# A four-layer kernel on one core: small TensorE groups placed one tile of the code search behind their producers

## The chip, the cores and the metric

The kernel runs on one core of a Trainium2 chip. The metric is the device time of one execution in microseconds (us). A core has five engines that matter here, each with its own queue, worked through in order: TensorE (PE, with PEld for its weight loads), VectorE (DVE), ScalarE (ACT), GpSimd (POOL) and SyncE (SP), which issues DMAs. Engines wait for each other by semaphores. An instruction that waits holds up everything behind it on its engine.

## What is computed

The input x has 16 images of 64 x 64 tokens with 256 channels. Four layers follow, each of the form x = x + L(group norm of x); the group norm has 32 groups of 8 channels and takes its mean and variance over a whole image.

```
L0: code search.  d = |x|^2 + |e|^2 - 2 x.e for 1024 codes e; take the nearest code's row
L1: per image row of 64 tokens: f = x Wf, g = x Wg, h = x Wh; out = sigmoid(f g^T) h
L2: x0, x1, x2 = x.w1, x.w2, x.w3 (one number a token);
    gate = sigmoid(sum_n x2[n] softmax_n(x0[n] x1[m]))[m]; out = gate * x
L3: linear attention with 4 heads of 32: softmax of q over a head, of k over the tokens,
    context = k^T v, out = layernorm(context q w_out)
```

## The kernel before

An image (4096 tokens, 256 channels as 2 halves of 128) is cut into 8 chunks of 512 tokens; the code search cuts a chunk into 4 tiles of 128 tokens, so an image has 32 tiles. Work on several images runs at once: while image b is searched, image b-1 is in layer 1, and earlier ones in layers 2 and 3. Each stage is a Python generator. A heap at the end of the kernel (function tile_net_kernel, at the foot) gives each generator a start in units of images and a length, and steps the one that is due; what a step yields is its share of the length. This makes the order in which instructions are *traced*. A scheduler then orders them by priority and by the buffers and engines that it takes to be free; a block under high_priority(offset=URGENT) goes ahead of what was traced up to 3000 places earlier. So the order on an engine is not the order of the text.

What the change and the prediction touch, with the lines of the kernel before:

- **gn_finish** (L259 to L282) closes a group norm. It runs four times an image: kind n0 (before the search), n1 (before layer 1), n2 (before layer 2), n3 (before layer 3), always under URGENT and in one step. DVE combines the statistics of the chunks into mv (L264). PE forms two sums in the bank pg (L268, L269) from the mean; ACT squares one into d (L271); PE forms the variance in pv from mv (L273) and from d (L274); ACT makes scale and nmean (s, L276; nm, L278); POOL raises s to the power -1/2 (L279) and forms nb (L281). For n0 three filler matmuls (function busy, L133) stand ahead of pg; their result is overwritten.
- **stage1**, the code search (L310 on). norm (L326) makes of a chunk, on ACT, the normalized tokens xn (L331) and their squares sq (L334): two instructions each. PE sums the squares over the channels into px (L340, 8 matmuls: four blocks of 32 partitions); ACT copies px to xrow (L345); PE turns xrow into pxt (L347), one transpose. norm_rows (L350) copies the four columns needed from pxt to nx2 on DVE (L352; nx in the profile). The search of a tile: ACT makes nn = -|e|^2 - |x|^2 (L381, from nx2); PE makes pd = 2 x.e, 1024 columns, in four matmuls (L386); DVE adds nn and takes the maximum into m8 (L392) and finds its place (L397); POOL gathers the code's row with an indirect DMA that adds it onto the tokens xc (L398). back (L357) transposes a chunk of the finished tokens (pt, L361), ACT copies it out (L364), DVE takes its statistics (L257). Within a chunk norm of the next chunk follows tile 2, norm_rows tile 3, and back of the last chunk tile 1.
- **rows2** (L550 on) prepares layer 2. Under URGENT, three filler matmuls (L133) go to the bank pbr, ACT scales the three weight vectors into wrow (L557), PE forms their bias (pbr, L562), ACT keeps it (L566). Then, for each half of the image, PE makes the three numbers of 2048 tokens in pr (L576), ACT adds the bias (rows, L580), ACT issues three DMAs that write them to DRAM, PE turns the rows (prt, L585: four transposes), and DVE copies two columns into x01 (L586; x_r in the profile). spread_rows (L591) loads the rows from DRAM, spread over the partitions, as x0b and x2b.
- **stage2** works on these: ACT's exponentials ex (L628, 2.09 us each) and DVE's weighted sums (L631, 2.32 us each), 64 of each an image. They are the costliest groups on their engines.
- layer1: ph (L476), psc, po (L516) on PE and the sum xt_l on DVE (L521). stage3: pk (L745), pqv (L762), ek, pc, pz (L835), pxo (L874) on PE.

Buffers: pd, ph and po share two double banks of PSUM; all other PSUM tiles share four single banks. Three SBUF buffers with the tag t4 are shared by nn, sq, fg of layer 1, and rows.

Of the kernel before, what the change touches and what calls it, by code (L numbers as in the profile page):

```python
# [41 lines left out]
def kernel(  # L42
# [212 lines left out]
    def chunk_stats(st, xt, ch):  # L255
        for k in range(NK):
            nc.vector.bn_stats(st[:, k, ch, :], xt[:, k, :])  # L257

    def gn_finish(st, kind, b):  # L259

        tag = f"{kind}_{b}"
        mv = small.tile([P, NK, 2], F32, tag="gn_mv", name=f"mv_{tag}")
        for k in range(NK):
            nc.vector.bn_aggr(mv[:, k, :], st[:, k, :, :].rearrange("p c s -> p (c s)"))  # L264
        mean = mv[:, :, 0]
        pg = bank(f"pg_{tag}")
        busy(pg, 3 if kind == "n0" else 0)
        nc.tensor.matmul(pg[:, 0:NK], lhsT=dmat, rhs=mean, start=True, stop=True)  # L268
        nc.tensor.matmul(pg[:, NK : 2 * NK], lhsT=gmat, rhs=mean, start=True, stop=True)  # L269
        d2 = small.tile([P, NK], F32, tag="gn_d", name=f"d_{tag}")  # L270
        nc.scalar.activation(d2, pg[:, 0:NK], AF.Square)  # L271
        pv = bank(f"pv_{tag}")
        nc.tensor.matmul(pv[:, 0:NK], lhsT=gmat, rhs=mv[:, :, 1], start=True, stop=False)  # L273
        nc.tensor.matmul(pv[:, 0:NK], lhsT=gmat, rhs=d2, start=False, stop=True)  # L274
        scale = small.tile([P, NK], F32, tag=f"gn_s{kind}", name=f"s_{tag}", bufs=3)
        nc.scalar.activation(scale, pv[:, 0:NK], AF.Identity, bias=eps5)  # L276
        nmean = small.tile([P, NK], F32, tag=f"gn_nm{kind}", name=f"nm_{tag}", bufs=3)
        nc.scalar.activation(nmean, pg[:, NK : 2 * NK], AF.Copy, scale=-1.0)  # L278
        nc.gpsimd.tensor_tensor(scale, scale, mhalf[:, 0:NK], ALU.pow)  # L279
        nbias = small.tile([P, NK], F32, tag=f"gn_nb{kind}", name=f"nb_{tag}", bufs=3)  # L280
        nc.gpsimd.tensor_tensor(nbias, nmean, scale, ALU.mult)  # L281
        return scale, nmean, nbias  # L282
# [9 lines left out]


    norm0 = {}

    def stats0(b):
# [3 lines left out]
        for ch in range(NCHUNK):  # L300
# [3 lines left out]
            yield 1.5  # L304
        with tc.high_priority(offset=URGENT):
            norm0[b] = gn_finish(st, "n0", b)
        yield 2
# [4 lines left out]
    def stage1(b):  # L312
# [3 lines left out]
        tok = x[b].rearrange("(t p) c -> p t c", p=P)  # L316
        xt, xc, xn, nx2, pxt = {}, {}, {}, {}, {}

# [8 lines left out]
        def norm(ch):  # L327
            xn[ch] = s1p.tile([P, NK, CW], F32, tag="xn", name=f"xn_{tag}_{ch}")
            sq = s1p.tile([P, NK, CW], F32, tag="t4", name=f"sq_{tag}_{ch}", bufs=3)
            for k in range(NK):  # L330
# [4 lines left out]
                    sq[:, k, :], xt[ch][:, k, :], AF.Square, bias=nbias[:, k : k + 1], scale=scale[:, k : k + 1]  # L335
                )
            px = bank(f"px_{tag}_{ch}")
            for t in range(CH):
                for k in range(NK):
                    nc.tensor.matmul(  # L340
                        px[32 * t : 32 * t + 32, :P], lhsT=neg32, rhs=sq[:, k, t * P : (t + 1) * P],
                        start=(k == 0), stop=(k == NK - 1),
                    )
            xrow = small.tile([P, P], F32, tag="xrow", name=f"xrow_{tag}_{ch}", bufs=1)
            nc.scalar.copy(xrow, px[:, :P])  # L345
            pxt[ch] = bank(f"pxt_{tag}_{ch}")
            nc.tensor.transpose(pxt[ch][:, :P], xrow, ident)  # L347

        def norm_rows(ch):
            px = pxt.pop(ch)  # L350
            nx2[ch] = small.tile([P, CH], F32, tag="x2", name=f"nx2_{tag}_{ch}")
            nc.vector.tensor_copy(nx2[ch], px[:, :P].rearrange("p (t n) -> p t n", n=32)[:, :, 0])  # L352
# [4 lines left out]
        def back(ch):  # L357
            for k in range(NK):
                pt = bank(f"pt_{tag}_{ch}_{k}")
                for t in range(CH):  # L360
                    nc.tensor.transpose(  # L361
                        pt[:, t * P : (t + 1) * P], xc[ch][:, t, k * P : (k + 1) * P], ident
                    )
                nc.scalar.copy(xt[ch][:, k, :], pt)  # L364
# [6 lines left out]
        load(1)  # L371
        norm(0)
        norm_rows(0)
        tokens(0)
        yield 4
        for ch in range(NCHUNK):
            for t in range(CH):
# [5 lines left out]
                for hf in range(2):  # L383
                    cols = slice(hf * 512, (hf + 1) * 512)
                    for k in range(NK):
                        nc.tensor.matmul(  # L386
                            pd[:, cols], lhsT=xn[ch][:, k, t * P : (t + 1) * P], rhs=e2[:, k, cols],
                            start=(k == 0), stop=(k == NK - 1),
                        )

# [12 lines left out]
                yield 4  # L403
                if t == 1 and ch > 0:
                    back(ch - 1)
                    yield 2
                if t == 2 and ch + 1 < NCHUNK:
                    norm(ch + 1)
                    yield 2
# [6 lines left out]
        back(NCHUNK - 1)  # L416
        with tc.high_priority(offset=URGENT):
            norm1[b] = gn_finish(st1, "n1", b)
        yield 3
# [4 lines left out]
    def layer1(b):  # L424
# [117 lines left out]

        with tc.high_priority(offset=URGENT):
            norm2[b] = gn_finish(st2, "n2", b)
        yield 2
# [4 lines left out]
    def rows2(b):  # L550
        tag = f"r2_{b}"
        scale, nmean, _ = norm2[b]
        with tc.high_priority(offset=URGENT):
            pb = bank(f"pbr_{tag}")
            busy(pb, 3)
            for k in range(NK):
# [3 lines left out]
                )  # L560
            for k in range(NK):
                nc.tensor.matmul(  # L562
                    pb[:, 0:1], lhsT=wrow_n[:, k, :], rhs=nmean[:, k : k + 1], start=(k == 0), stop=(k == NK - 1)
                )
            brow_n = small.tile([P, 1], F32, tag="brow_n", name=f"brow_{tag}")
            nc.scalar.activation(brow_n, pb[:, 0:1], AF.Identity, bias=brow)  # L566
        x01 = small.tile([P, NT, 2], F32, tag="x01", name=f"x01_{tag}", bufs=2)
        rd = dram.tile([3, 2, 4, CW], F32, tag="rows", name=f"rows_{tag}", bufs=3)
        for h in range(2):
            pr = bank(f"pr_{tag}_{h}")  # L570
            for j in range(4):
# [3 lines left out]
                for k in range(NK):  # L575
                    nc.tensor.matmul(  # L576
                        pr[part, :], lhsT=wrow_n[:, k, part], rhs=xt[:, k, :], start=(k == 0), stop=(k == NK - 1)
                    )
            rows = s1p.tile([P, CW], F32, tag="t4", name=f"rows_{tag}_{h}", bufs=3)
            nc.scalar.activation(rows, pr, AF.Identity, bias=brow_n)  # L580
            for n in range(3):
                nc.scalar.dma_start(out=rd[n, h], in_=rows[n : n + 97 : 32, :])
            pt = bank(f"prt_{tag}_{h}")
            for t in range(CH):
                nc.tensor.transpose(pt[:, t * P : (t + 1) * P], rows[:, t * P : (t + 1) * P], ident)  # L585
            nc.vector.tensor_copy(  # L586
                x01[:, 16 * h : 16 * h + 16, :].rearrange("p (j t) n -> p j t n", t=CH),
                pt.rearrange("p (t j n) -> p j t n", j=4, n=32)[:, :, :, 0:2],
            )
            yield 4  # L590
        rows_d[b] = x01, rd, [spread_rows(rd, b, 0)]  # L591
# [72 lines left out]
    def gate2(b):  # L664
# [9 lines left out]
        for ch in range(NCHUNK):  # L674
# [16 lines left out]
            nc.sync.dma_start(out=dst[ch], in_=xt)  # L691
        with tc.high_priority(offset=URGENT):
            scale, nmean, _ = gn_finish(st3, "n3", b)
        norm3[b] = scale, nmean, xm_
# [264 lines left out]
```

## Time and profile before

| | us |
|---|---|
| three runs | 5700.67, 5725.21, 5726.86 (median 5725.21) |
| the profiled execution | 5709.26 |
| its span | 5707.6 |
| steady stretch used below | 1400 to 4900 |
| matmuls pd, 4096 in all | 2008.5 busy, 0.625 each |
| sums ex, 1024 in all | 2364.2 busy on DVE, 2.315 each |
| exponentials ex, 1024 in all | 2137.9 busy on ACT, 2.088 each |
| squares and normalized tokens, 256 each | 0.80 each on ACT |
| filler matmuls, 96 in all | 0.38 each |

How to read it: a row of waits, "A line <- B line: us, times, longest", is the time in which engine A stood idle until that instruction of B ended. A row of the timeline gives start, length, engine, line, operation, out<-in, and in brackets the idle time before it and what ended it. A table of stretches gives, for each piece of the span, each engine's busy time and (x) instructions, then the granted clock of PE as a share of the full one. The profile counts two matmuls where the program has one on float32 data.

### The profile page before, as it was taken

The page shows a single profiled execution, that of the slowest core. Times are in us where ns is not written, and L with a number is a line of the kernel's source. Part 1 is how long each engine was busy: PE and PEld are TensorE (multiplying, and loading weights), DVE is VectorE, ACT ScalarE, POOL GpSimd, SP SyncE. Part 2 cuts the span into 40 slices and gives each one's busy share as a digit, 9 for nine tenths or more (in the row PEclk, how much of TensorE's full clock was granted, in tenths as well). Part 3 has the DMA queues.
Part 4 walks back from the last instruction along what each step waited for, and adds up shares of the span by engine and source line. Part 5 has one row for each costly group of instructions (what it writes and reads, how often), then busy time and mean ns, then how long its engine had stood idle before and what let it go on. Part 6 is the DMA issues. An engine that isn't in the chain of part 4 may idle for free.

```text
span 5707.6 us, 71918 instructions
## 1 busy us (share of the span) xinstructions
PE 5070.7 (89%) x24911; PEld 2999.1 (53%) x24911; DVE 5046.3 (88%) x7186; ACT 4578.7 (80%) x6578; POOL 1929.1 (34%) x1203
## 2 busy tenths in 40 slices
PE   8978899889999999999989999899999999997777
PEld 3534455445555565554645555564555545564444
DVE  6489798999999999998999999999898998988982
ACT  4478587978889798887978888798887878888873
POOL 3123233323333334334333333333333333321332
PEclk9988999989999999999999999999999999997888
DMA  6453835655666757566575756757475674745544
GB/s 187 141 158 93 265 112 188 176 161 177 191 188 176 212 160 198 175 190 186 170 205 163 187 188 177 203 161 218 143 193 172 184 207 142 203 153 160 158 137 92
DMA packets 453763, 991.87 MB, mean 174 GB/s; under 512 B 50456, under 2 KB 198808, under 8 KB 445208
## 3 DMA queue, kind: packets, MB, share of 16 engines
q1 hardware_dynamic: 320272, 750.88, 39.7%
q0 software_dynamic: 92160, 134.26, 15.5%
q10 hardware_dynamic: 40968, 102.13, 4.6%
q8 instruction: 198, 3.24, 0.2%
q14 instruction: 165, 1.35, 0.1%
HBM read 684.07 MB, written 303.04 MB: 173 GB/s over the span
## 4 chain that ended last, share of the span: by engine, by line
PE 34%; DVE 19%; ACT 13%; issue 6%; POOL 3%; DMA 3%; ACTq 0%; SPq 0%; POOLq 0%; DVEq 0%
PE pd_s L386 11%; DVE ex_s L631 7%; ACT ex_s L628 6%; PE ph_l L476 3%; DVE i_s L397 3%; PE pqv_s L762 2%; PE pxo_s L874 2%; PE pk_s L745 2%; ACT nn_s L381 2%; DVE nn_s L392 2%; POOL qv_s L780 1%; PE po_l L516 1%; PE pz_s L835 1%; DVE st_s L257 1%; DVE xg_g L686 1%
## 5 line engine op out<-in xcount | busy, mean ns | idle before, releaser
L631 DVE CUSTOM_DVE_ANT_0 ex_s<-ex_s,x2b 128x2048 f32<-128x2048 f32 x1024 | 2364.2, 2315 | 77.0 <-ACT ex_s L628 75.1
L628 ACT ACTIVATE ex_s<-x0b,nmax_s,x_r 128x2048 f32<-128x2048 f32 x1024 | 2137.9, 2088 | 80.8 <-DVE num_s L631 77.8
L386 PE MATMUL pd_s<-e,xn_s 128*128 128x512 f32 x4096 | 2008.5, 625 | 71.6 <-DVE m L392 61.5
L398 POOL DMA_INDIRECT xc_s<-in_emb_rows,i_s x512 | 1160.6, 2267 | 1794.2 <-DVE i_s L397 1255.3
L386 PEld LDWEIGHTS pd_s<-e,xn_s 128*128 128x128 f32 x4096 | 763.4, 198 | 855.4 <-issue 705.3
L392 DVE CUSTOM_DVE_ANT_0 nn_s<-pd_s,nn_s 128x1024 f32<-128x1024 f32 x512 | 619.7, 1213 | 137.4 <-PE pd_s L386 100.5
L381 ACT ACTIVATE nn_s<-ne,nx_s 128x1024 f32<-128x1024 f32 x512 | 580.4, 1143 | 55.9 <-DVE nx_s L352 27.5
L397 DVE FIND_INDEX8 i_s<-m,nn_s 128x8 uint32<-128x1024 f32 x512 | 623.5, 1219 | 0.0
L476 PE MATMUL ph_l<-wh_l,xt_l 128*128 128x256 f32 x2048 | 536.1, 399 | 68.0 <-DVE xt_l L521 42.6
L762 PE MATMUL pqv_s<-wqv_s,xk_s 128*128 128x256 f32 x2048 | 488.7, 380 | 0.0
L476 PEld LDWEIGHTS ph_l<-wh_l,xt_l 128*128 128x128 f32 x2048 | 386.6, 196 | 193.1 <-issue 65.9
L762 PEld LDWEIGHTS pqv_s<-wqv_s,xk_s 128*128 128x128 f32 x2048 | 388.7, 191 | 120.2 <-issue 59.8
L780 POOL TENSOR_TENSOR qv_s<-qv_s,qm_s 128x512 f32<-128x512 f32 x128 | 216.1, 1688 | 640.0 <-DVE qm_s L779 329.3
L874 PE MATMUL pxo_s<-qo_s,wctx_s 128*128 128x512 f32 x512 | 279.5, 630 | 18.5 <-DVE qo_s L854 18.1
L736 POOL TENSOR_TENSOR qv_s<-qv_s,qd_s 128x512 f32<-128x512 f32 x128 | 186.1, 1454 | 324.7 <-DVE qd_s L735 189.8
L516 PE MATMUL po_l<-blk,h_l 128*128 128x128 f32 x2048 | 286.1, 291 | 3.6 <-DVE m L392 2.9
L516 PEld LDWEIGHTS po_l<-blk,h_l 128*128 128x128 f32 x2048 | 263.1, 202 | 42.2 <-issue 22.8
L884 POOL DMA_DIRECT2D out<-y_s x128 | 118.9, 929 | 479.3 <-ACT lrs_s L845 235.2
L745 PE MATMUL pk_s<-xk_s,wk_s 128*128 128x512 f32 x512 | 259.0, 626 | 0.0
L846 POOL TENSOR_TENSOR lrs_s<-lrs_s,mhalf 128x4 f32<-128x4 f32 x128 | 199.0, 1555 | 173.1 <-ACT lrs_s L845 164.2
L361 PE MATMUL pt_s<-ident,xc_s 128*128 128x128 f32 x1024 | 157.6, 289 | 103.6 <-DMA xc_s<-in_emb_rows,i_s 70.0
L875 ACT ACTIVATE y_s<-pxo_s,xm_g 128x512 f32<-128x512 f32 x256 | 174.6, 683 | 91.3 <-PE pxo_s L874 90.6
(191 smaller groups left out, 7012.6 us busy)
## 6 DMA issues: line engine op xcount, KB each, us to landing
xs_s<-in_xT SPq DMA_DIRECT2D x128, 512.0 KB
xt_s<-in_xT SPq DMA_DIRECT2D x128, 512.0 KB
xc_s<-in_x SPq DMA_DIRECT2D x128, 512.0 KB
x_s<-xt_s ACTq DMA_DIRECT2D x128, 512.0 KB
xt_l<-x_s SPq DMA_DIRECT2D x128, 512.0 KB
x_l<-xt_l SPq DMA_DIRECT2D x128, 512.0 KB
xr_r<-x_l SPq DMA_DIRECT2D x128, 512.0 KB
xg_g<-x_l SPq DMA_DIRECT2D x128, 512.0 KB
```

The costliest lines, as they stand in the source:

```text
L381: nc.scalar.activation(nn, ne2, AF.Identity, bias=nx2[ch][:, t : t + 1])
L386: nc.tensor.matmul(pd[:, cols], lhsT=xn[ch][:, k, t * P : (t + 1) * P], rhs=e2[:, k, cols], start=(k == 0), stop=(k == NK - 1),)
L392: nc.vector.tensor_tensor_reduce(out=nn, in0=pd, in1=nn, scale=1.0, scalar=-3.0e38, op0=ALU.add, op1=ALU.max, accum_out=m8[:, 0:1],)
L397: nc.vector.max_index(i8, m8, nn)
L398: nc.gpsimd.indirect_dma_start(out=xc[ch][:, t, :], out_offset=None, in_=emb_rows, in_offset=bass.IndirectOffsetOnAxis(ap=i8[:, 0:1], axis=0),
L476: nc.tensor.matmul(ph[:, t, :], lhsT=X[:, k, t * P : (t + 1) * P], rhs=wh_n[:, k, :], start=(t % 2 == 0 and k == 0), stop=False, skip_grou ...
L516: nc.tensor.matmul(po[:, m : m + P], lhsT=h[:, t, k * P : (k + 1) * P], rhs=at[:, t, :, :].rearrange("p r i -> p (r i)"), start=True, stop ...
L628: nc.scalar.activation(ex, x0b, AF.Exp, bias=nmax[:, T : T + 1], scale=x01[:, T, 1:2], accum_out=den[:, h, T : T + 1])
L631: nc.vector.tensor_tensor_reduce(out=ex, in0=ex, in1=x2b, scale=1.0, scalar=0.0, op0=ALU.mult, op1=ALU.add, accum_out=num[:, h, T : T + 1],)
L745: nc.tensor.matmul(pk, lhsT=wk_n[:, k, :], rhs=xt[:, k, :], start=(k == 0), stop=(k == NK - 1))
L762: nc.tensor.matmul(pqv[:, j, :], lhsT=xt[:, k, t * P : (t + 1) * P], rhs=wqv_n[:, k, :], start=(j == 0 and k == 0), stop=False, skip_group ...
L874: nc.tensor.matmul(px, lhsT=wctx[:, 1, pr * P : (pr + 1) * P], rhs=qT, start=True, stop=True)
```

## The change

Three kinds of PE groups are pinned. The last search matmul traced so far is kept in marks["search"]; a block under behind("search") may not be put ahead of that matmul in PE's order, whatever its priority. Their work is also cut into more steps, so that between a producer on another engine and the PE group that reads it a step of the heap passes.

- Token norms: norm follows tile 1 (before: tile 2), px with its copy xrow becomes a step of its own (norm_sums) after tile 2, the transpose pxt moves into norm_rows after tile 3. back is pinned too.
- Group norms: gn_finish becomes a generator with two pauses, one after mv and one after d; urgently() runs each step under URGENT, but not what other stages trace in between. Each kind gets its own small buffers mv and d.
- Layer 2's rows: weights, bias, rows and their turning are steps of their own; the rows get two buffers of their own in place of a t4 buffer.
- The 96 filler matmuls, with their weight loads, are gone. Apart from these the two programs hold the same number of instructions of each kind on each engine, DMAs included; only semaphore instructions differ.

```diff
+    def urgently(gen):
+        while True:
+            with tc.high_priority(offset=URGENT):
+                try:
+                    step = next(gen)
+                except StopIteration as end:
+                    return end.value
+            yield step
...
+    marks = {}
+    def behind(name):
+        return tc.issue_after(marks[name]) if name in marks else nullcontext()
...
     def gn_finish(st, kind, b):
...
+        yield 1.5
         mean = mv[:, :, 0]
         pg = bank(f"pg_{tag}")
-        busy(pg, 3 if kind == "n0" else 0)
-        nc.tensor.matmul(pg[:, 0:NK], lhsT=dmat, rhs=mean, start=True, stop=True)
-        nc.tensor.matmul(pg[:, NK : 2 * NK], lhsT=gmat, rhs=mean, start=True, stop=True)
+        with behind("search"):
+            nc.tensor.matmul(pg[:, 0:NK], lhsT=dmat, rhs=mean, start=True, stop=True)
+            nc.tensor.matmul(pg[:, NK : 2 * NK], lhsT=gmat, rhs=mean, start=True, stop=True)
...
         nc.scalar.activation(d2, pg[:, 0:NK], AF.Square)
+        yield 1.5
...
+        with behind("search"):
+            nc.tensor.matmul(pv[:, 0:NK], lhsT=gmat, rhs=mv[:, :, 1], start=True, stop=False)
+            nc.tensor.matmul(pv[:, 0:NK], lhsT=gmat, rhs=d2, start=False, stop=True)
...
-        with tc.high_priority(offset=URGENT):
-            norm1[b] = gn_finish(st1, "n1", b)
+        norm1[b] = yield from urgently(gn_finish(st1, "n1", b))
...
+        def norm_sums(ch):
+            sq = sqs.pop(ch)
             px = bank(f"px_{tag}_{ch}")
...
+            with behind("search"):
+                for t in range(CH):
+                    for k in range(NK):
+                        nc.tensor.matmul(
...
         def norm_rows(ch):
-            px = pxt.pop(ch)
+            px = bank(f"pxt_{tag}_{ch}")
+            with behind("search"):
+                nc.tensor.transpose(px[:, :P], xrows.pop(ch), ident)
...
-                        nc.tensor.matmul(
+                        marks["search"] = nc.tensor.matmul(
                             pd[:, cols], lhsT=xn[ch][:, k, t * P : (t + 1) * P], rhs=e2[:, k, cols],
                             start=(k == 0), stop=(k == NK - 1),
-                        )
+                        ).ins
...
-                if t == 1 and ch > 0:
-                    back(ch - 1)
+                if t == 1:
+                    if ch + 1 < NCHUNK:
+                        norm(ch + 1)
+                    if ch > 0:
+                        back(ch - 1)
                     yield 2
                 if t == 2 and ch + 1 < NCHUNK:
-                    norm(ch + 1)
+                    norm_sums(ch + 1)
                     yield 2
...
     def rows2(b):
...
-            busy(pb, 3)
...
+        yield 1
+        with tc.high_priority(offset=URGENT):
+            pb = bank(f"pbr_{tag}")
+            with behind("search"):
+                for k in range(NK):
...
+        def turn(h):
+            pt = bank(f"prt_{tag}_{h}")
+            with behind("search"):
+                for t in range(CH):
+                    nc.tensor.transpose(pt[:, t * P : (t + 1) * P], rows[h][:, t * P : (t + 1) * P], ident)
...
-            rows = s1p.tile([P, CW], F32, tag="t4", name=f"rows_{tag}_{h}", bufs=3)
-            nc.scalar.activation(rows, pr, AF.Identity, bias=brow_n)
+            rows[h] = s1p.tile([P, CW], F32, tag="rows", name=f"rows_{tag}_{h}", bufs=2)
+            nc.scalar.activation(rows[h], pr, AF.Identity, bias=brow_n)
...
-            yield 4
+            yield 2
+            turn(h)
+            yield 1
```

## The prediction

> **What bounds the kernel now.** I read the head of the page, then the table of stretches, then the waits by engine in the steady stretch, then single stalls.
>
> ```profile
> span 5707.6 us, 71918 instructions
> PE 5070.7 (89%) x24911; PEld 2999.1 (53%) x24911; DVE 5046.3 (88%) x7186; ACT 4578.7 (80%) x6578; POOL 1929.1 (34%) x1203
> ```
>
> No engine is full over the span, but the ends dilute this. The steady stretch 1400 to 4900 us (some 10.4 images of about 336 us) reads, in the table of stretches (columns: length; busy time and instructions of PE, PEld, DVE, ACT, POOL; granted clock, DMA share, GB/s):
>
> ```profile
> 1400.00:4900.00 3500.00, 3219.35 (x16199) 1925.73 (x16201) 3249.82 (x4616) 2966.27 (x4261) 1286.67 (x766) 0.96 0.63 183
> ```
>
> DVE is busy 93%, PE 92% at a clock of 0.96. Both are near full, and DVE's instructions stay the same in number and kind: the time of this stretch is DVE's 3250 us plus its idle 250 us, and the change can only alter the second term. The waits of DVE, in us, times and longest, say who owns it:
>
> ```profile
> DVE ex_s L631 <- ACT ex_s L628: 53.8, 32, 3.9
> DVE qd_s L734 <- ACT qv_s L781: 45.8, 12, 5.7
> DVE nkm_s L748 <- PE pk_s L745: 32.3, 30, 2.4
> DVE qz_s L837 <- PE pz_s L835: 26.0, 39, 1.4
> DVE nn_s L392 <- PE pd_s L386: 19.6, 12, 3.1
> DVE nn_s L392 <- ACT nn_s L381: 18.1, 26, 1.4
> ```
>
> With the smaller rows PE owns 102 us (32.3 + 26.0 + 19.6 + ctxbd 9.8, qo 6.2, ctx 5.0, four small ones 2.8), ACT 124 us, POOL's powers in the norms 22 us. None of these rows names an instruction that the change pins; they are what is late because PE and ACT stood still earlier. PE's own waits in the same stretch:
>
> ```profile
> PE ph_l L476 <- DVE xt_l L521: 42.6, 28, 3.4
> PE pd_s L386 <- DVE m L392: 37.3, 27, 3.0
> PE px_s L340 <- ACT sq_s L334: 35.3, 27, 2.2
> PE pg_n L268 <- DVE mv_n L264: 25.9, 8, 4.5
> ...
> PE prt_r L585 <- ACT rows_r L580: 18.2, 7, 2.6
> PE pxt_s L347 <- ACT xrow_s L345: 13.3, 23, 1.5
> ```
>
> px, pxt, pg, prt (and pbr, 7.8) are the pinned groups: 100.5 of PE's 281 us of idle time. A stall costs more than its length. The timeline has one, and slices of 2 us around it show the granted clock:
>
> ```profile
> 2799.39 0.41 PE L340 MATMUL px_s<-sq_s,neg 128*32 128x128 f32 x2 [1.77 <-ACT sq_s L334]
> ```
> ```profile
> 2798.00:2800.00 2.00, 0.61 (x4) 0.41 (x5) 2.00 (x4) 2.00 (x4) 1.45 (x1) 1.00 1.06 408
> 2800.00:2802.00 2.00, 2.00 (x12) 2.00 (x11) 2.00 (x3) 1.98 (x4) 0.13 (x1) 0.51 1.01 320
> 2802.00:2804.00 2.00, 1.60 (x17) 0.85 (x16) 1.48 (x4) 0.52 (x2) 0.00 (x0) 0.63 0.34 74
> 2804.00:2806.00 2.00, 2.00 (x21) 1.21 (x21) 1.31 (x5) 2.00 (x4) 0.71 (x1) 1.00 0.53 197
> ```
>
> After 1.77 us of idle PE runs at half clock for about 4 us: 0.98 + 0.74 = 1.7 us lost on top. I cut two periods (2770 to 3110, 3850 to 4190) into such slices: 25.6 us of clock lost, 6.8 us of it behind px stalls (four times), 5.1 us behind pg stalls (twice). The stretch loses 0.04 x 3500 = 140 us by its mean clock of 0.96.
>
> **The change, part by part.** Where the order matters I compare the order in which the two built programs hold their instructions, pricing the PE and DVE work between two of them by the mean rows of the groups.
>
> 1. *Token norms.* norm (4 ACT instructions of 0.80 us a chunk) moves one tile earlier; px goes behind the matmuls of tile 2, pxt behind those of tile 3. PE work between the squares and px rises from 0 (median) to 10.6 us, and between px and pxt from 0.87 to 5.3 us. A tile lasts 336/32 = 10.5 us, so the ACT queue has time: px's 35.3 and pxt's 13.3 us go, and the clock behind px, 6.8/25.6 x 140 = 37 us. ACT's copy xrow, which waited 40.0 us in the stretch for px, stood directly behind it (0 us of ACT work between); now 1.35 us lies between on average. I take three quarters, 30 us.
>
> 2. *Turned rows and bias row.* rows to prt: 0.4 to 4.4 us of PE work, over the longest wait of 2.6; prt's 18.2 us go. wrow to pbr: 0.3 to 4.75 us, against waits up to 1.5; 7.8 us go. The three DMAs of each half stay on ACT's queue directly behind their activation, and the loads of x0b are issued after the last step as before, so the stage of exponentials has no later start. The rows get their own two buffers and leave one of the three that nn, sq and fg share.
>
> 3. *Group norms.* The step is cut by two pauses, each sum pinned. n0 and n3 already had 8 to 22 us of cover. The long pg stalls, one an image, are n1 at the turn from one image to the next. There the pin changes little: PE work between the last transposes and pg rises from 1.74 to 3.48 us (images 8 to 14), while DVE has 3.46 us to do up to mv (5.24 before) and ACT two copies of 0.58. Seven long stalls make 25.6 us, 3.7 each. Bounds: nothing gained (DVE stays that far behind) to 25.6; I take the added cover, 7 x 1.74 = 12 us, and half of the clock behind pg, 14 of 5.1/25.6 x 140 = 28 us. d and s stay directly behind their sums on ACT: nothing gained there. Later scales: n3's sums get some 10 us more PE work before them; layer 3 is due 0.04 of an image, 13 us, after the gate, so I cost it at nothing; without that cover it would be those 10 us once, at the last image, since the others overlap.
>
> 4. *Fillers.* 96 bf16 matmuls go, 32 groups of three; the chain of waits gives such a group 0.65 us. 21 groups lie in the stretch: 14 us. They also kept PE from idling. The trace has no row without them; bounds for their loss are 0 and, if each place became a px-like clock drop, 21 x 1.7 = 36 us. I take 0: 0.65 us of work is short beside the 1.77 us stall, and the waits behind it are the ones removed. The Trainium skill (TensorE: Matmul & The Clock Gate, Part 1: The HAM clock gate) speaks against dropping fillers, and says that an idle window of about 3.4 us halves the clock; here 1.77 us did, so the measurement decides. By the page only pg stalls would cost clock, 37 us of my clock term would be missing, and the gain below would be 9 us smaller.
>
> *The sum.* PE loses 281 + 140 = 421 us in the stretch. Removed: 35.3 + 13.3 + 18.2 + 7.8 + 12 = 87 idle, 37 + 14 = 51 clock, 14 fillers: 152, or 36%. I let the DVE idle that PE owns shrink in proportion: 0.36 x 102 = 37 us. ACT is idle 534 us and gets 30 back, 6%: 0.06 x 124 = 7 us. Against it stands the first tile of a chunk: nx is read off pxt, nn waits for it, and DVE's sum waits for nn. DVE work between nn's place and its use falls there from a median of 1.30 to 0.10 us, but rises for the second and fourth tile (3.6 to 5.4, 3.9 to 7.1). Places with under 1.2 us fall from 34% to 23% over all tiles, so I leave the 18.1 us as they are. Net 44 us in 3500, 1.26%; over 700 to 4900 us that is 53. Before 700 us I add 5 (DVE waited 26 us for pxt in the first image, in part by a late load); behind 4900 us the search ends, pins cost nothing and gain nothing. 5709 - 58 = 5651 us on the profiled execution (5709.3, span 5707.6). The median shown, 5725, is 16 us above it, and the three runs span 5701 to 5727; I place the forecast between, at **5660 us**.
>
> **Rivals.** The bound for what this measurement can tell from no change is 0.5%, 29 us: faster is under 5697, slower over 5754.
>
> *The wait moves on (no change).* PE, freed of px, comes sooner to matmuls that wait for DVE: ph and pd already wait 42.6 + 37.3 + 21.6 = 101.5 us for xt, m and their PSUM buffers. For it: DVE is 93% busy and fully busy in the slices of the stall above, so PE's pause cost DVE nothing at once. Against: DVE later stands 102 us for PE, so the pauses are not all absorbed. Then only ACT's 7 us remain: 5725 - 8, about 5717.
>
> *The late first tile (slower).* The squares now hold one of the three shared buffers over 15 us of DVE work instead of 3, and nx comes after pxt, which stands 5.1 us of PE work behind tile 3 (before: 0.4 ahead of its end). If nn of the first tile is exposed in full, 1.14 us on each of 128 chunks, that is 146 us: 5667 + 146 = 5813. It cancels the gain from 58/128 = 0.45 us a chunk, and is slower by the bound from 0.68 us. For it: the lead of 0.10 us. Against: the other tiles lead by more, and the waits on ACT nn are now 0.7 us each.
>
> *Everything DVE waits for PE goes (larger gain).* 102 + 22 us in 3500 and 5 before, scaled: 149 + 5; 5571 at the median's level, 5555 at the profile's. It needs ACT to keep pace.
>
> **How the numbers follow.** Forecast (5600 to 5697) 0.50, larger gain 0.06, wait moves on 0.24, late first tile 0.20. So faster 0.56, same 0.24, slower 0.20; the forecast's own range is 5600 to 5697. The range 5585 to 5785 leaves out about 0.05 below and 0.1 above; it takes in the open bounds of pg (12 us more or less) and of the fillers (36 us).
>
> **What would show it.** px, pxt, prt and pbr vanish from PE's waits; ACT's wait for px falls to 10 us or less; the steady clock rises from 0.96 to about 0.975; pg <- mv stays, at half; DVE's idle share in the stretch falls from 7.1% to about 6%. If PE's idle is unchanged and ph and pd wait longer, the wait moved on. If nn_s <- ACT nn_s or ACT's nn <- nx grows past 60 us, the first tile is late. The forecast is wrong if the pauses of PE were hidden behind DVE after all, or if the shared buffer turns ACT into the late engine.

## The result and the profile after

The changed kernel takes **5757.16 us** (median of 8 runs, 5745.25 to 5776.74); the kernel before took 5708.36 us beside it. The ratio is **1.0089, interval 1.0072 to 1.0106**: slower by 0.9%, where 5660 us and faster had been forecast. The profiled execution took 5776.74 us, the longest of the 8 and 20 us over their median, so differences read between the traces come out somewhat larger than the ratio. Its page begins:

```profile
span 5775.0 us, 71662 instructions
PE 5022.3 (87%) x24815; PEld 2989.4 (52%) x24815; DVE 5058.4 (88%) x7186; ACT 4562.1 (79%) x6578; POOL 1973.9 (34%) x1203
```

PE has 48 us less to do (31 of it the fillers, L133: 16.9 and 13.7 us in the trace of before; the 0.38 us given above is the median of one, and in a group they overlap), DVE 12 more, and the span has grown by 67. The table of stretches for 1400 to 4900 us (columns as before):

```profile
1400.00:4900.00 3500.00, 3127.25 (x15845) 1877.61 (x15844) 3208.77 (x4543) 2900.60 (x4189) 1286.68 (x752) 0.95 0.61 180
```

DVE does 73 instructions fewer in the same 3500 us: it is idle 291 us instead of 250. The granted clock fell from 0.96 to 0.95; 0.975 had been expected. DVE's waits in the stretch (us, times, longest):

```profile
DVE nkm_s L783 <- PE pk_s L780: 61.8, 13, 8.1
DVE ex_s L667 <- ACT ex_s L664: 45.4, 33, 3.3
DVE gate_s L681 <- ACT gate_s L680: 36.9, 10, 5.1
DVE wqv_s L304 <- POOL s_n L292: 29.9, 10, 4.3
DVE nn_s L417 <- ACT nn_s L406: 28.0, 33, 2.8
...
DVE nx_s L375 <- PE pxt_s L373: 12.6, 10, 1.9
```

The first row has doubled (32.3 before) and has another shape: 13 long waits instead of 30 short ones, about one an image. PE's waits:

```profile
PE pd_s L411 <- DVE m L417: 101.8, 46, 5.0
PE ph_l L503 <- DVE xt_l L548: 67.4, 11, 6.3
PE pt_s L385 <- DMA xc_s<-in_emb_rows,i_s: 37.7, 16, 5.0
PE pxo_s L909 <- DVE qo_s L889: 31.1, 10, 3.5
PE pgt_s L685 <- DVE gate_s L682: 30.1, 10, 4.4
PE pk_s L780 <- DMA xk_s<-out: 24.2, 10, 4.3
```

Of the five pinned groups that the forecast counted only 13.9 us of px are left, of 100.5: there the pins do what they say. It left out two that are pinned too: pv, which now waits 14.8 us (none before), and back's pt, with 37.7 us (32.1 before). And PE's waits altogether went from 278 to 371 us, and those for DVE from 138 to 243.

**Where the time was lost.** I took the start of the operation in which DVE adds nn and takes the maximum (L417) for each of the 512 tiles and averaged over ten images. Against the run norows below (all of the change but layer 2's part) chunks 0 to 5 of the search agree within 0.9 us each; chunk 6 takes 37.8 instead of 33.8 us, chunk 7 38.7 instead of 36.4. That is where layer 2's rows are made, and where layer 3 of an earlier image begins.

### The profile page after: what moved, and what is told of

Read it like the earlier page. It is cut to its first block, busy times and chain, and to the rows that moved or that the text cites. A ratio compares the mean times of both kernels' runs of the same rounds, so it can differ in the third digit from the quotient of the medians.

```text
span 5775.0 us, 71662 instructions
## 1 busy us (share of the span) xinstructions
PE 5022.3 (87%) x24815; PEld 2989.4 (52%) x24815; DVE 5058.4 (88%) x7186; ACT 4562.1 (79%) x6578; POOL 1973.9 (34%) x1203
## 5 line engine op out<-in xcount | busy, mean ns | idle before, releaser
L423 POOL DMA_INDIRECT xc_s<-in_emb_rows,i_s x512 | 1136.1, 2219 | 2146.3 <-DVE i_s L422 1431.7
L411 PEld LDWEIGHTS pd_s<-e,xn_s 128*128 128x128 f32 x4096 | 777.6, 202 | 1035.3 <-issue 804.0
L417 DVE CUSTOM_DVE_ANT_0 nn_s<-pd_s,nn_s 128x1024 f32<-128x1024 f32 x512 | 620.8, 1213 | 145.4 <-PE pd_s L411 72.4
L815 POOL TENSOR_TENSOR qv_s<-qv_s,qm_s 128x512 f32<-128x512 f32 x128 | 192.9, 1507 | 432.3 <-DVE qm_s L814 303.4
L771 POOL TENSOR_TENSOR qv_s<-qv_s,qd_s 128x512 f32<-128x512 f32 x128 | 224.5, 1754 | 311.6 <-DVE qd_s L770 148.5
L909 PE MATMUL pxo_s<-qo_s,wctx_s 128*128 128x512 f32 x512 | 290.9, 654 | 39.0 <-DVE qo_s L889 37.8
L780 PE MATMUL pk_s<-xk_s,wk_s 128*128 128x512 f32 x512 | 284.1, 682 | 31.9 <-DMA xk_s<-out 31.9
L349 ACT ACTIVATE xn_s<-xt_s,nb_n,s_n 128x512 f32<-128x512 f32 x256 | 201.6, 806 | 139.1 <-DMA xt_s<-in_xT 105.5
L881 POOL TENSOR_TENSOR lrs_s<-lrs_s,mhalf 128x4 f32<-128x4 f32 x128 | 263.9, 2061 | 105.6 <-ACT lrs_s L880 94.3
L543 PEld LDWEIGHTS po_l<-blk,h_l 128*128 128x128 f32 x2048 | 252.6, 195 | 37.8 <-issue 26.7
L543 PE MATMUL po_l<-blk,h_l 128*128 128x128 f32 x2048 | 266.5, 281 | 4.3 <-DVE m L417 4.0
```

Of the source, the lines that this page charges most:

```text
L411: marks["search"] = nc.tensor.matmul(pd[:, cols], lhsT=xn[ch][:, k, t * P : (t + 1) * P], rhs=e2[:, k, cols], start=(k == 0), stop=(k == N ...
L417: nc.vector.tensor_tensor_reduce(out=nn, in0=pd, in1=nn, scale=1.0, scalar=-3.0e38, op0=ALU.add, op1=ALU.max, accum_out=m8[:, 0:1],)
L423: nc.gpsimd.indirect_dma_start(out=xc[ch][:, t, :], out_offset=None, in_=emb_rows, in_offset=bass.IndirectOffsetOnAxis(ap=i8[:, 0:1], axis=0),
L543: nc.tensor.matmul(po[:, m : m + P], lhsT=h[:, t, k * P : (k + 1) * P], rhs=at[:, t, :, :].rearrange("p r i -> p (r i)"), start=True, stop ...
L780: nc.tensor.matmul(pk, lhsT=wk_n[:, k, :], rhs=xt[:, k, :], start=(k == 0), stop=(k == NK - 1))
L909: nc.tensor.matmul(px, lhsT=wctx[:, 1, pr * P : (pr + 1) * P], rhs=qT, start=True, stop=True)
```

## The experiments

All ratios stand against the kernel before on the same chip, with their 95% intervals. DVE's idle time in the stretch, added up from the rows of waits by the engine that ended it, tells the runs apart best:

| run | ratio | PE | ACT | POOL | all |
|---|---|---|---|---|---|
| before | 1 | 102 | 124 | 22 | 249 |
| tok | 1.0006 | 45 | 157 | 40 | 242 |
| norows | 0.9979 | 45 | 154 | 41 | 241 |
| changed kernel | 1.0089 | 104 | 146 | 39 | 288 |
| after_pbr | 1.0013 | 94 | 114 | 53 | 262 |
| after_y0 | 0.9961 | 80 | 115 | 43 | 238 |

**First theories.** A: the pins do as they say, and the loss comes with other work that the scheduler moves, most of it with the token norms. B: the late first tile. C: the missing fillers. Four runs have one part of the change each.

**tok**: the token norms' part of the diff (norm one tile earlier, norm_sums, pinned px, pxt and back).

> The kernel before with the token norms alone changed (norm after tile 1, sums after tile 2, transpose after tile 3, these and back pinned); group norms, rows and fillers as before. Theory A, the pins do what they say and the loss comes from other work that the scheduler moves with them: px and pxt stalls go (35 and 13 us of the steady stretch), but this part carries most of the whole loss of 0.9%: ratio 1.004 to 1.012, with DVE waiting for the exponential of the gate (some 40 us in all), since in the built order no DVE work stands any more between that exponential and the addition that reads it. Theory B, the late first tile of a chunk: ratio over 1.005 with the waits of DVE for nn and of ACT for nx grown by over 60 us together. Theory C, the fillers carry the loss: ratio 0.985 to 0.998, since they are kept here.

1.0006 (0.9995 to 1.0017): no loss and no gain. B falls (nn waits 2.3 us an image for ACT, 1.9 before), and A's place was wrong.

**gn**: gn_finish with its pauses and pins; fillers kept.

> The kernel before with the group norms alone changed (two pauses, sums pinned); the fillers stay. Theory A: the built order keeps the same gate, the same n1 cover of 1.74 us and the same token norms, so 0.997 to 1.003. If the finer steps of the group norms carry the loss: 1.005 or more, with POOL's scales later and DVE waiting longer for s. Theory C: as theory A.

0.9995 (0.9983 to 1.0008): no loss here either.

**rows**: rows2 alone, pbr's fillers kept.

> The kernel before with the rows of layer 2 alone changed (own steps, pinned, own buffers); fillers stay. prt's 18 us and pbr's 8 us in the steady stretch go in any case. Theory A: the gate's addition keeps little DVE work before it (0.2 us against 1.3), so a part of the gate stall appears: 0.996 to 1.006. Theory B: no loss, 0.993 to 1.000, since nn keeps its lead. Theory C: 0.993 to 1.000.

**1.0166** (1.0143 to 1.0189), worse than the whole change. DVE's waits in the stretch of this run:

```profile
DVE nkm_s L765 <- PE pk_s L762: 53.7, 28, 6.7
...
DVE ctx_s L804 <- PE pc_s L802: 48.4, 16, 6.1
DVE nn_s L398 <- ACT nn_s L387: 43.3, 34, 6.0
```

All three have grown (32.3, 5.0 and 18.1 before), the first two by work of layer 3.

**nofill**: only the two busy calls removed.

> The kernel before without the 96 filler matmuls, nothing else; its built order is that of before in all measured distances. Theory C, fillers hold the clock: ratio 1.004 to 1.010 and the steady clock 0.01 lower. Theories A and B: 0.996 to 1.001 (14 us of matmuls less on PE in the steady stretch).

1.0007 (0.9996 to 1.0018); the granted clock of the whole span is 0.942, and 0.941 with them. C falls.

So the loss sits in the part on layer 2's rows. The next theory, **L**, said *lateness*: the pauses make the sums pr, the turning and what follows late. One suspect was the maximum ab on POOL, which in rows comes 8 us of DVE work behind the last exponential sum of the image before, and ahead of it before. Rival P: the pins and cuts themselves; rival G: the norms' parts.

**norows**: the changed kernel, rows2 as before (without fillers).

> The changed kernel with its part on layer 2's rows undone: token norms, group norms and the removal of the fillers stay. Theory L (lateness): the new pauses in rows2 make the sums pr, the turned rows and the loads behind them later; in the changed kernel the loads xk of layer 3 then come late behind them on SP's queue and DVE stands 5.6 us an image for pk at the 26th tile of the search. Without that part this stall is gone: 1.000 (0.996 to 1.003), pk's stall under 1 us an image. Rival G (the pins or pauses of the norms cost, alone or together, what the changed kernel lost): 1.007 to 1.010, the stall stays.

**0.9979** (0.9965 to 0.9993). G falls: without the part on the rows the change is a small gain.

**rows_short** and **after_short**: the length of the rows stage, in rows and in the changed kernel.

```diff
-        task("rows", end + LAGR, 0.1, rows2(b), 8)
+        task("rows", end + LAGR, 0.06, rows2(b), 8)
```

> Layer 2's rows part alone, as in the run rows (1.0166), but the stage is given 0.06 of an image instead of 0.10, so that its steps, as many and as pinned as there, come up to 0.035 of an image (12 us) earlier. Theory L: the cost is the lateness of the maximum over x01 on POOL (ab), which stands some 8 us of DVE work behind the last sum of the image before in the run rows and 12 us ahead of it here; the time comes back to 0.998 to 1.003 and chunk 7 of the search from 48.3 to about 40 us. Rival P (what costs is the pinning and cutting itself, the groups standing behind search matmuls, or the two buffers of their own): nothing of this is changed, so 1.012 to 1.017.

1.0091 (1.0066 to 1.0116): half the loss stays, so neither L nor P as stated.

> The changed kernel in full, with the rows stage given 0.06 of an image instead of 0.10. Theory L: the sums pr of the first half give their buffers back some 10 us earlier, SP gets to the loads xk earlier, DVE's 5.6 us for pk at tile 26 go: 0.997 to 1.003 (5690 to 5727 us). If the pinned norms were worth what was forecast and only the lateness hid it: 0.988 to 0.995. Rivals G and P: unchanged, 1.007 to 1.010.

1.0002 (0.9989 to 1.0015): in the changed kernel the time is as L said, though DVE's wait for pk is halved (5.9 to 3.0 us an image) and not gone.

**late**: the kernel before with LAGR = 0.05 in place of 0.03.

> The kernel before with one number changed: the rows stage starts 0.05 instead of 0.03 of an image behind layer 1, 6.7 us later; no pin, no pause, no buffer. Theory L: the lateness by itself costs it: in the built order ab moves from 9.5 us of DVE work ahead of the last sum of the image before to 7.5 us behind it, as in the run rows, so 1.008 to 1.02, lost in chunk 7 of the search. Rival P: no cut and no pin, so 0.998 to 1.003.

1.0005 (0.9987 to 1.0022). ab comes late here as in rows, and nothing is lost: that suspect falls. What differs from rows is SP's order: in late layer 3's first load xk is issued 18.2 us after DVE starts on tile 22 of the search (of 32, counted from 0; the recorded texts call it the 22nd), ahead of the rows' loads; in rows at 44.1 us, behind them (31.8 before).

**Theory Q, read from the trace.** Loads xr (layer 2's rows) and xk (layer 3) share four buffers, and SP issues them in order. The second half's four xr wait until PE's sums pr of the first half give the buffers back, and xk comes behind, when the second half's sums give them back again. One image of the changed kernel, timeline of all engines (start, length, engine, line, what, and in brackets the idle time before):

```profile
3305.11 0.50 ACT L581 ACTIVATE wrow_n<-wrow_raw,s_n 128x12 f32<-128x12 f32 x2 [0.57 <-POOL s_n L292]
3308.20 5.35 PE L411 MATMUL pd_s<-e,xn_s 128*128 128x512 f32 x8 [3.62 <-DVE m L417]
3313.39 0.50 PE L590 MATMUL pbr_r<-nm_n,wrow_n 128*128 128x1 f32 x4
3313.82 1.94 PE L617 MATMUL pr_r<-xr_r,wrow_n 128*32 128x512 f32 x16
3315.75 1.75 SPq L614 DMA_DIRECT2D xr_r<-x_l  x4
3325.51 0.32 SPq L634 DMA_DIRECT2D x0b<-rows_r  x1
3325.92 0.93 SPq L775 DMA_DIRECT2D xk_s<-out  x1
3334.60 2.92 PE L780 MATMUL pk_s<-xk_s,wk_s 128*128 128x512 f32 x4 [3.64 <-DMA xk_s<-out]
3337.56 0.69 DVE L783 TENSOR_REDUCE nkm_s<-pk_s 128x1 f32<-128x512 f32 x1 [5.98 <-PE pk_s L780]
```

Read it downwards. The weights wrow are ready at 3306. The bias group pbr, 0.50 us long, is pinned behind a search matmul that waits 3.62 us for DVE to free its PSUM bank and then runs 5.35 us. pr, whose last load was issued 30 us earlier (3283.36), stands behind pbr. Only when pr ends does SP get on. DVE stands 5.98 us ahead of nkm, at the end of the chain; the index search and the sum ex that it does directly behind nkm stand after it in DVE's order. The same in norows, where pbr is free:

```profile
3263.27 0.50 ACT L582 ACTIVATE wrow_n<-wrow_raw,s_n 128x12 f32<-128x12 f32 x2 [0.56 <-POOL s_n L292]
3267.37 0.58 PE L587 MATMUL pbr_r<-nm_n,wrow_n 128*128 128x1 f32 x4
3267.88 1.94 PE L601 MATMUL pr_r<-xr_r,wrow_n 128*32 128x512 f32 x16
3269.82 1.75 SPq L598 DMA_DIRECT2D xr_r<-x_l  x4
3277.97 0.32 SPq L623 DMA_DIRECT2D x0b<-rows_r  x1
3289.49 0.33 SPq L764 DMA_DIRECT2D xk_s<-out  x1
3293.41 1.88 PE L769 MATMUL pk_s<-xk_s,wk_s 128*128 128x512 f32 x4
3296.26 0.69 DVE L772 TENSOR_REDUCE nkm_s<-pk_s 128x1 f32<-128x512 f32 x1
```

From weights to pr it is 4.6 us instead of 8.7, and xr, x0b and xk come well apart. In the changed kernel the DMA engines first stand almost idle and then take all three in one burst (last columns: clock, DMA share, GB/s):

```profile
3304.00:3315.00 11.00, 7.38 (x29) 3.58 (x31) 10.85 (x14) 7.91 (x13) 5.85 (x5) 0.84 0.12 28
3315.00:3335.00 20.00, 15.39 (x63) 6.40 (x56) 14.87 (x21) 14.03 (x19) 4.31 (x5) 1.00 0.93 304
```

Over ten images, in us. The first three columns count from the start of DVE's work on tile 22; DVE's work is counted between the issue of xk and the first nkm:

| run | pr starts | x0b issued | xk issued | xk to end of pk | DVE work meanwhile | DVE waits for pk |
|---|---|---|---|---|---|---|
| norows | 13.6 | 24.8 | 35.6 | 6.2 | 5.2 | 0.1 |
| norows_pin | 17.7 | 29.2 | 35.5 | 9.0 | 6.7 | 1.3 |
| changed kernel | 18.3 | 30.7 | 33.5 | 9.6 | 3.7 | 5.6 |
| after_pbr | 13.8 | 22.7 | 34.0 | 8.5 | 5.7 | 2.2 |
| after_y0 | 13.0 | 22.2 | 33.9 | 7.4 | 7.1 | 0.3 |

So xk itself is not issued later in the changed kernel (33.5 us, against 34.0 in after_pbr). What comes later with pr is x0b, 2.8 us ahead of xk instead of 11.3. Against after_pbr pk is done 1.1 us later after the issue of xk, and DVE has 2.0 us less work to cover it: the shorter cover is the larger part of the difference, and no run changes the cover alone.

**after_y0**: the changed kernel with weights, bias and first half in one step again.

```diff
-        yield 1
         with tc.high_priority(offset=URGENT):
             pb = bank(f"pbr_{tag}")
...
             nc.scalar.activation(brow_n, pb[:, 0:1], AF.Identity, bias=brow)
-        yield 1
...
             turn(h)
-            yield 1
+            yield 2
```

> The changed kernel without its two pauses ahead of the rows' first half (weights and bias again in the step of the first half); the pins, the own buffers, the delayed turning and all other parts stay. Theory Q (a queue of loads): SP's four loads xr of the second half wait for the buffers that the sums pr of the first half hold, and the loads xk of layer 3 stand behind them. In the changed kernel these pr start 18.3 us after the 22nd tile (12.8 to 13.6 in the runs without the rows part), SP stands still until then, and xr, x0b, x2b and xk then come in one burst. Without the pauses pr stands 8 us earlier in PE's built order: 0.997 to 1.003, pk's stall from 5.9 us an image to under 2. Rival P (the pins and the delayed turning cost): 1.006 to 1.010, stall unchanged.

**0.9961** (0.9945 to 0.9977): faster than both kernels, a little better than Q's range. No search tile is traced any more between weights and bias, so the pin costs no place. Two rows of DVE's waits in its stretch:

```profile
DVE x_r L603 <- PE prt_r L602: 40.7, 10, 5.0
...
DVE nkm_s L781 <- PE pk_s L778: 4.6, 3, 2.1
```

Of pk's 61.8 us 4.6 are left; the wait for the turned rows is 28 us longer (40.7, against 12.2 in the changed kernel).

**norows_pause**: norows with the two pauses alone, as three lines (two `yield 1`, and `yield 3` for the halves' `yield 4`).

> From the other side: the run norows (0.9979) with nothing of the rows part but the two pauses; no pin, turning in the same step, old buffers. In the built order pr of the first half keeps its early place here, while the loads xk move 5 us of DVE work later. Theory Q in its strict form (it is pr's place that decides): 0.997 to 1.002. Rival A (any pause in rows2 that makes xk later costs it): 1.005 to 1.010 with pk's stall at 3 us or more. Rival P (pins and turning): 0.997 to 1.000.

0.9979 (0.9966 to 0.9992). Pauses alone cost nothing.

**after_spread**: x0b and x2b issued before the first turning.

```diff
             yield 2
+            if h == 0:
+                halves = [spread_rows(rd, b, 0)]
             turn(h)
```

> The changed kernel with the loads x0b and x2b of the first half issued before its turning, not behind the last step of the stage. Nothing of pr's place changes. Theory Q: SP is held by pr as before, and the two loads now stand ahead of xr: no gain, 1.006 to 1.013. Rival B (the burst is the cost: 2 MB of x0b and x2b beside xk): the burst is broken up, pk's stall falls under 3 us, 0.998 to 1.004.

**1.0183** (1.0161 to 1.0205). The wait for pk fell to 2.5 us an image, as this run's rival B said, and the time rose all the same. But the burst was not broken up: x0b is issued 30.2 us after tile 22 instead of 30.7, x2b 30.9 instead of 33.9, and from xk's issue to the end of pk it is 11.6 us instead of 9.6. The wait is shorter because DVE has 9.2 us of work meanwhile. So the run does not test B; what it shows is that a shorter wait for pk need not shorten the time. The loss is larger than Q's range, too; qd and nn wait more for ACT (5.2 and 4.3 us an image).

**rows_y0**: rows without its pauses.

> The rows part alone (rows: 1.0166, in a stage of 0.06: 1.0091) without its two pauses. Here pr of the first half stands no earlier than in those two, but the second half's pr and the loads xk do. Theory Q: some of the loss comes back, 1.004 to 1.010; if the pauses were the whole of it, 0.998 to 1.003; rival P (pins, delayed turning): 1.012 to 1.017.

1.0170 (1.0145 to 1.0195): missed. What rows loses alone is not its pauses.

**after_pbr**: one pin off.

```diff
-            with behind("search"):
+            with nullcontext():
                 for k in range(NK):
                     nc.tensor.matmul(
                         pb[:, 0:1], lhsT=wrow_n[:, k, :], rhs=nmean[:, k : k + 1], start=(k == 0), stop=(k == NK - 1)
                     )
```

> The changed kernel with one pin of its many taken off: that of the two bias matmuls of layer 2 (pbr). Pauses, delayed turning, own buffers and all other pins stay. In the built order pr of the first half then stands 10.2 instead of 18.2 us of DVE work behind the 22nd tile. Theory Q: 0.995 to 1.002, DVE's wait for pk from 5.9 us an image to under 2, pr 13 to 15 us behind the tile instead of 18.3. Rival P (the delayed turning, the own buffers, or the sum of all pins): 1.006 to 1.010.

**1.0013** (1.0003 to 1.0024): in this kernel one pin on two matmuls is worth 0.0076 of the 0.0089. pr is back at 13.8 us; DVE's waits in its stretch:

```profile
DVE x_r L605 <- PE prt_r L604: 23.8, 10, 2.9
DVE nkm_s L783 <- PE pk_s L780: 16.5, 10, 3.6
```

The wait for the gate (36.9 us in the changed kernel) shrank to 0.3 us an image too; the runs don't tell why.

**norows_pin**: norows_pause with that same pin put on.

> From the other side: the run norows_pause (0.9979) with one pin more, that of the two bias matmuls; nothing else of the rows part. In the built order only pbr, pr of the first half and the loads behind it move, by 8 us of DVE work. Theory Q: 1.005 to 1.012, DVE's wait for pk at 3 us an image or more (1.6 in norows_pause), pr 17 us or more behind the 22nd tile (12.1). Rival P: 0.997 to 1.000.

1.0003 (0.9992 to 1.0014), 0.0024 above norows_pause, where the interval ends at 0.9992: missed by Q (1.005 to 1.012), with the right sign and a third of the pin's 0.0076. pr is nearly as late as in the changed kernel (17.7 us), but DVE has 6.7 us of work to cover 9.0, and waits as little as without the pin. By this row the late pr costs much only where the cover is short.

**after_nopin**: the changed kernel, all pins off.

> The changed kernel with no pin at all; steps, pauses, moved norm, buffers and the missing fillers stay. pr of the first half stands early (10.2). Theory Q: no loss, 0.995 to 1.003. If the pins of the token norms and group norms are worth what the forecast gave them, this one is slower than after_pbr by 0.005 or more; if the steps alone take the groups off PE's waits, the two agree within 0.003 and PE's waits px, pxt and pg are as small here as in the changed kernel.

1.0083 (1.0066 to 1.0100): missed by Q. pk's wait is small (0.6 us an image), but x_r, nn and st (DVE for PE, ACT, ACT) have 3.8, 3.8 and 3.0. So the other pins are worth 0.7% against after_pbr, as this run's second sentence allowed; the loss here shows in other waits than that of the changed kernel.

**after_xk**, **y0_xk**, **norows_xk**: the first xk issued at the top of stage3, in the changed kernel, after_y0 and norows.

```diff
+        xk = {}
+        def fetch(ch):
+            xk[ch] = xb.tile([P, NK, CW], F32, tag="xb", name=f"xk_{tag}_{ch}")
+            nc.sync.dma_start(out=xk[ch], in_=x3[ch])
+        fetch(0)
         wk_n = wts.tile([P, NK, P], F32, tag="wk_n", name=f"wk_{tag}")
...
-            xt = xb.tile([P, NK, CW], F32, tag="xb", name=f"xk_{tag}_{ch}")
-            nc.sync.dma_start(out=xt, in_=x3[ch])
+            if ch > 0:
+                fetch(ch)
+            xt = xk.pop(ch)
```

> The changed kernel with every pin, pause and late pr in its place; only layer 3's first load xk of an image is issued at the top of its stage, ahead of the weights, so that on SP's queue it stands ahead of the four loads xr that wait for pr instead of behind them. The wait of DVE for pk was 5.6 us an image: from the issue of xk to the end of pk 9.6 us, with 3.7 us of DVE work to cover them. Theory Q (the load behind the rows' loads is the cost): the wait falls under 1.5 us, 0.996 to 1.003. Rival R (the reordered work on DVE and PE around it is the cost, the load only its place): the time moves to other waits, 1.005 to 1.010.

**1.0116** (1.0086 to 1.0146): above the ranges of both Q and R. The wait for the first pk fell to 0.8 us an image, as Q said. But xk now holds one of the four buffers, the fourth xr comes late, and the turned rows with it. SP's and DVE's waits in the stretch:

```profile
SPq L741 <- PE pr_r L617: 140.9, 20, 15.6
```

```profile
DVE x_r L605 <- PE prt_r L604: 51.8, 10, 7.2
DVE nkm_s L791 <- PE pk_s L788: 44.5, 24, 2.9
```

The second half's pr ends 42.3 us after tile 22 instead of 33.7, and DVE waits 51.8 us for prt instead of 12.2. My reading, which no further run tests: the buffers, given back late, set the time, and whichever load stands last pays.

> The run after_y0 (0.9961, pk's wait 0.3 us an image) with the same early load. Theory Q: there is nothing left to take, 0.994 to 0.998; more than that would mean that the early load gains elsewhere too. Rival R: 0.994 to 1.000, any other order may cost.

1.0052 (1.0034 to 1.0069): above both ranges, a loss where nothing was left to take; what grew most is DVE's wait for ACT's ex (9.9 instead of 4.1 us an image).

> The run norows (0.9979, pk's wait 0.1 us an image) with the same early load. Theory Q: 0.996 to 1.000, nothing left to take. Rival R: 0.997 to 1.003.

0.9962 (0.9948 to 0.9977): as good as after_y0, the best of all runs with it.

## Why the prediction was wrong

**The step that failed: "Turned rows and bias row".** It weighed pbr's pin against PE's own wait for wrow (7.8 us in the stretch, gone as said) and concluded "so the stage of exponentials has no later start". It looked at one consumer. Behind pbr on PE stands pr; pr gives back the buffers for which SP's loads xr wait; behind those stand x0b and layer 3's xk. The pin moved pr some 5 us back (13.8 to 18.3, and 12.1 to 17.7). The working never looked at SP's queue for this edit. Put in the forecast's terms, part 2 was booked as a saving of 18.2 + 7.8 us of PE idle, some 6 us of DVE's, and is worth +0.0110 of the time (norows to the changed kernel), some 60 us the other way. The sentence on the exponentials fails too: x0b is issued 30.7 us after tile 22 (27.3 before), and the image's first exponential starts at 67.1 us (58.4 before). That alone is not the loss: in after_pbr it starts at 66.3.

That the pin together with the pauses carries the loss of this kernel is shown by two runs: without this pin 1.0013, without the two pauses ahead of the rows 0.9961. That it reaches DVE through SP's loads and pk (61.8 us in the stretch, 2.6 in norows) is read from the trace and shown in part only: after_spread, after_xk and after_nopin brought the wait for pk down to 2.5, 0.8 and 0.6 us an image and still took 1.0183, 1.0116 and 1.0083.

**The step that failed second: the proportion.** "I let the DVE idle that PE owns shrink in proportion: 37 us." In norows it shrank by 57 us, from 102 to 45: more than forecast. But ACT's share was to fall by 7 and rose by 31 (124 to 154), and POOL's rose by 19 (22 to 41). Net DVE gained 8 us in the stretch, not 44, and the run 0.2%, not 1%. Here the removal of the waits that ended last exposed the next ones. The largest are ex (63.3 us in norows, 53.8 before), the power in layer 3's scale (31.3, 6.7 before) and the gate (22.5, no row before). A slip without weight: the "four small ones" in the sum of PE's 102 us are three rows.

```profile
DVE ex_s L656 <- ACT ex_s L653: 63.3, 39, 2.6
DVE wqv_s L304 <- POOL s_n L292: 31.3, 10, 4.1
DVE gate_s L670 <- ACT gate_s L669: 22.5, 10, 3.6
...
DVE nkm_s L772 <- PE pk_s L769: 2.6, 3, 1.6
```

**The rival "the wait moves on"** describes the norms' parts: tok 1.0006, gn 0.9995, norows 0.9979, all within the bound. It named PE's waits for DVE as the place, and they did grow (138 to 206 us in norows), but DVE's idle time did not grow with them; what took back the gain was DVE's waiting for ACT and POOL. It did not see the rows.

**The clock.** Forecast 0.975, measured 0.95 in norows and in the changed kernel. PE now stops less often, but for longer: the trace of before has 222 stalls in the stretch, 4 of them over 3.4 us (16 us together); norows has 177, 37 of them over 3.4 us (182 us). Around one of 6.33 us (ph starts at 3128.59 in norows) the slices read:

```profile
3124.00:3126.00 2.00, 0.00 (x0) 0.00 (x0) 2.00 (x5) 2.00 (x2) 0.74 (x1) 1.00 0.74 156
3126.00:3128.00 2.00, 0.00 (x0) 0.00 (x0) 2.00 (x4) 2.00 (x3) 2.00 (x1) 0.76 0.42 166
3128.00:3130.00 2.00, 1.41 (x3) 1.17 (x4) 2.00 (x5) 2.00 (x3) 0.23 (x1) 0.50 0.32 129
3130.00:3132.00 2.00, 2.00 (x7) 1.54 (x6) 2.00 (x6) 1.68 (x4) 0.00 (x0) 0.50 0.33 133
3132.00:3134.00 2.00, 2.00 (x10) 1.36 (x10) 2.00 (x2) 0.92 (x2) 0.87 (x1) 0.53 0.55 190
```

PE is idle, DVE busy throughout (third figure), and the clock stays at 0.5 until 3134. The Trainium skill (TensorE: Matmul & The Clock Gate, Part 1: The HAM clock gate) ties the halving to an idle window of about 3.4 us. In the trace of before a stall of 1.77 us had been followed by 0.51, and the trace decides here; still, by a count of the long stalls the change should lose clock, and it did. My term went by the short ones alone.

**Right:** of the five pinned groups counted, four left PE's waits and px kept 13.9 us; fillers at nothing (1.0007); group norms, booked at some 6 us or 0.1%, 0.9995. xrow's wait on ACT fell from 40.0 to 19.0 us, 21 of the 30 us that had been forecast. **The late first tile** did not come as a loss (tok 1.0006): DVE's wait for ACT's nn is 28.0 us in the changed kernel (18.1 before) and ACT's wait for nx 34.8 (5.3 before), both under the 60 named; DVE also waits 12.6 us for pxt (1.2 before).

**What stays open.** The rows' part alone loses 1.7% with and without its pauses, and half of that in a shorter stage; its waits spread over pk, pc, nn and ex, and no run isolates one of them. Nor is it settled why the gate waits longer in the changed kernel, or what exactly the order loses without any pin. norows_pin shows that the pin reaches its full effect only with the rest of the rows' part (delayed turning, own buffers); why DVE's cover is shorter there, and whether the burst of loads costs by itself, no run tells.

## What to carry to other kernels

When a small group is held back in an in-order queue, ask first what stands behind it and which buffers that work gives back, then follow these through the DMA queue to the next stage, and look at how much work the bounding engine has there to cover a late load; the group's own wait may be the least of it. A wait that is removed is worth what the next waits leave: price a gain by the second latest arrival on the bounding engine, not by the share removed. If a pin is wanted for order, keep producer and pinned group in one step of the tracing, so that no other work comes between (after_y0, 0.9961, is this change with that repair).

## What the runs showed of the hardware

- In the stall above idle PE time that cost DVE nothing at once still cost clock: after the 6.33 us PE ran at half clock for about 6 us, under a DVE that never stopped.
- Four 512 KB loads and the 1 MB loads behind them, held back by 11 us in which the DMA share was 0.12 (28 GB/s), then ran at 0.93 (304 GB/s) for 20 us: the queue that had been held did not catch up at once. From issue to its matmul xk took 8.7 us in this burst, and 3.9 us in the image of norows, where it was issued 11.5 us behind x0b.
- POOL is idle 7.4 us on average ahead of its all-reduce ab (118 us, 16 times, in the trace of before) and again ahead of the next operation but the gathers (8.1 us in one image of before, 9.8 in one of rows). In the run late this came behind the last sum of an image, with no exponentials left to cover it, and cost nothing that the time shows.
